# First graph layer: four fewer row blocks held on chip, eight gathers a block instead of seven, twelve row buffers

## The chip, the cores and the metric

The program runs on one core of a Trainium2 chip. The core has five engines that run side by side and meet through semaphores: TensorE (PE; its weight loads are listed as PEld), VectorE (DVE), ScalarE (ACT), GpSimd (POOL) and SyncE (SP). In this kernel SP issues the plain DMA transfers, and POOL issues the indirect ones, in which 128 row numbers choose 128 rows of a table. The metric is the time of one execution on the device in microseconds (us), the median of several executions. Lower is better.

## The reference, cut to what matters

The program is a stack of four graph layers over 6250 nodes of 256 values and 100000 edges. Only the first layer is touched:

```python
h = jnp.einsum('nd,od->no', x, W) + b          # one row of 256 values for each node
row, col = (edge_index[0], edge_index[1])      # src, dst
msgs = h[col]                                  # the row of each edge's dst ...
out = jax.ops.segment_sum(msgs, row, num_segments=h.shape[0])   # ... summed at its src
x = _layernorm(x + out, axis=-1)
```

The edges come sorted by `dst`, and `dst` is drawn as 6250 times the square of a uniform number, so that low node numbers have many more edges than high ones. `src` is uniform.

## The kernel before, in words

Nodes are cut into 49 blocks of 128. A first phase (`prepare`, up to about 900 us) computes `h`, splits each row into two halves of 32-bit values whose sum is the row (512 values, 2 KB), writes the table `rows0` to HBM, and keeps the rows of the first 20 node blocks on chip in the tile `first_rows` (`FIRST = 20`). It also sorts the edges by the block of their source. Each source block gets 17 tiles of 128 edge places (`S_TILES`), in the order of `dst`. As `dst` is sorted, tile t of a block can only hold targets from a known range of node blocks, its window (`WINDOWS`), worked out beforehand.

The first layer is `direct_l0` (L1173), which calls `by_source` (L1077). For each source block the 17 tiles fall into two kinds.

- Near tiles are the leading ones whose window ends at or below block `h` (`near_tiles`). Their target rows are on chip, so no row is fetched. PE builds, for each target block, a 128x128 matrix of how many edges lead from each source to each target: one bf16 product of two one-hot matrices for each pair of a tile and a target block (L1134). Four such matrices fill one PSUM tile `ps_q`, a quad, which ACT copies to SBUF as `a_hi` (L1137). Then each matrix is multiplied with the 128 kept rows, once for each half (L989 and L990 in `sum_halves`), into the sum `ps_g`.
- Far tiles are the rest. For each, POOL gathers the 128 rows of its edges from `rows0` into a buffer `g` by an indirect DMA (L983, called at L1157), and PE multiplies them with the one-hot matrix of the edges' sources, `cs`, again once for each half.

The one-hot matrices of block b+1 are made by DVE in `open_block` while block b is under way, in this order: `od` (one for each near tile, L1096), `os` and `cs` (one instruction each, L978). All three have two buffers, so that those of block b+1 have to wait until PE has used up those of block b-1. After them in DVE's order stand the layer's ends: the sum with `x` (L1186), the layer norm (L962 to L972) and the split into halves (L945).

The order is written out by hand (`manual_schedule`). The unit of work is one quad. PE builds the quad two units ahead of the one whose products it runs (`stages(len(units), 2, build, use)`). In each unit the far tiles due come first (`range(q * m // n_q, (q + 1) * m // n_q)` of m far tiles over n_q quads), then the products with kept rows. POOL's gathers are issued in the order in which PE uses them. A gather waits until its buffer is free, that is until PE has used the gather that had the buffer before, and until the gather eight before it has landed, for there are eight completion semaphores for POOL's transfers.

With `H0 = 24` as the bound for near tiles, the rows of blocks 20 to 23 are read back from `rows0` into a tile `more_rows` by one transfer of 1 MB at the start of the layer (L1176, L1177). By the windows, a source block then has 10 near and 7 far tiles, 59 pairs of tile and target block, 24 target blocks and 6 quads (the last block of 106 nodes: 8 near, 9 far, 52 pairs, 23 target blocks, 6 quads).

When the layer ends, the last rows it made are read back into `first_rows` for the second layer (L1776), and the second layer, `direct_l1`, begins. It, the third (`direct_l2`, which uses `by_source` with `exact` set and 16 buffers for gathered rows) and the fourth (`direct_l3`) gather rows at the same line L983.

Of the kernel before, what the change touches and what calls it, by code (L numbers as in the profile page):

```python
# [7 lines left out]
FT = mybir.dt.float32  # L8
# [8 lines left out]
P = 128  # L17
# [33 lines left out]
S_TILES = sum(n for _, _, _, n in STRETCHES)  # L51
TS = NB * S_TILES
S_ROWS = -(-(S_TILES * P * NB + E) // P)
H0, H1, H2, H3 = 24, 16, 9, 3
SURE = 3.5


# [31 lines left out]
FIRST = 20  # L89
# [6 lines left out]
W0 = 2 * D  # L96
# [555 lines left out]
class Slots:  # L652
# [40 lines left out]
    def hot(self, dst, b, lo, hi):  # L693
        self.k.nc.vector.tensor_scalar(dst, self.sb[:, lo:hi], float(b), None, op0=OP.is_equal)
# [54 lines left out]
class Scores:  # L749
# [46 lines left out]
    def load(self, c):  # L796
        if c % self.STEP and c != EC or c > EC or c in self.at:
            return
        at = self.at[c] = self.pool.tile([P, self.STEP, DE], FT, name="at", bufs=2)
        if c < EC:  # L800
            n = min(self.STEP, EC - c)
            self.k.nc.sync.dma_start(at[:, :n, :],
                                     self.attr[c * P:(c + n) * P, :].rearrange("(c p) d -> p c d", p=P))
        else:
            self.k.nc.sync.dma_start(at[:ET, 0, :], self.attr[P * EC:E, :])
# [142 lines left out]
def load_block(k, pool, table, b, name="xb", bufs=3):  # L948

    t = pool.tile([P, D], FT, name=name, bufs=bufs)  # L950
    n = rows_of(b)
    if n < P:
        k.nc.vector.memset(t, 0.0)
    k.nc.sync.dma_start(t[:n, :], table[b * P:b * P + n, :])
    return t
# [14 lines left out]
def normalized(k, dst, x, mv, rs):  # L970
    k.nc.vector.reciprocal(rs, rs)
    k.nc.vector.tensor_scalar(dst, x, mv[:, 0:1], rs, op0=OP.subtract, op1=OP.mult)  # L972


def one_hots(k, dst, loc, op=OP.is_equal):

    n = loc.shape[-1]
    k.nc.vector.tensor_tensor(dst, k.iota_row.unsqueeze(1).to_broadcast([P, n, P]),  # L978
                              loc.unsqueeze(2).to_broadcast([P, n, P]), op=op)


def gather(k, dst, table, idx):
    k.nc.gpsimd.indirect_dma_start(out=dst, out_offset=None, in_=table,  # L983
                                   in_offset=bass.IndirectOffsetOnAxis(ap=idx, axis=0))


def sum_halves(k, out, lhs, row, start, stop):

    k.nc.tensor.matmul(out, lhs, row[:, :D].bitcast(F32R), start=start, stop=False)  # L989
    k.nc.tensor.matmul(out, lhs, row[:, D:2 * D].bitcast(F32R), start=False, stop=stop)  # L990
# [16 lines left out]
class Pairs:  # L1007
# [30 lines left out]
    def by_source(self, t):  # L1038
        return self.s[:, t - self.t0, :]


def stages(n, lag, make, use):

    made = {}
    for i in range(n + lag):
        if i < n:
            made[i] = make(i)
        if i >= lag:
            use(i - lag, made.pop(i - lag))
# [27 lines left out]
def by_source(k, pool, psum, hot, h, table, width, idx, loc, rel, load, finish, scale=None):  # L1077

    nc = k.nc
    near = [Near(b, h) for b in range(NB)]
    units = [(b, q) for b in range(NB) for q in range(len(near[b].quads))]
    nn, nf = max(v.n for v in near), S_TILES - min(v.n for v in near)
    pairs = max(v.pairs for v in near)
    exact = scale is not None
    sides, far, sums, later = {}, {}, {}, []

    def open_block(b):
        v, s = near[b], b * S_TILES
        od = pool.tile([P, pairs * P], BF16, name="od", bufs=2)
        for t, (lo, hi) in enumerate(v.spans):
            o = (v.at[t] + lo) * P
            nc.vector.tensor_scalar(od[:, o:o + (hi - lo) * P], k.iota16[:, :(hi - lo) * P], rel[:, s + t:s + t + 1],  # L1096
                                    None, op0=OP.is_equal)
        os = pool.tile([P, nn, P], BF16, name="os", bufs=2)
        one_hots(k, os[:, :v.n, :], loc[:, s:s + v.n])
        by_s = [os]  # L1100
        if exact:
            by_s = []
            for i, w in enumerate(scale[1]):
                by_s.append(pool.tile([P, nn, P], BF16, name=f"osw{i}", bufs=2))
                ws = w[:, s:s + v.n].unsqueeze(2).to_broadcast([P, v.n, P])
                nc.vector.tensor_tensor(by_s[i][:, :v.n, :], os[:, :v.n, :], ws, op=OP.mult)
        sides[b] = od, by_s
        m = S_TILES - v.n
        if exact:
            far[b] = []  # L1110
            for t in range(v.n, S_TILES):
                far[b].append(pool.tile([P, P], FT, name="cs", bufs=2 * nf))
                nc.vector.tensor_scalar(far[b][-1], k.iota_row, loc[:, s + t:s + t + 1], scale[0][:, s + t:s + t + 1],
                                        op0=OP.is_equal, op1=OP.mult)
        else:
            cs = pool.tile([P, nf, P], F32R, name="cs", bufs=2)
            one_hots(k, cs[:, :m, :], loc[:, s + v.n:s + S_TILES])
            far[b] = [cs[:, j, :] for j in range(m)]

    def build(i):  # L1120
        b, q = units[i]
        v = near[b]
        if q == 0:
            load(b)
            if b + 1 < NB:
                open_block(b + 1)
        od, by_s = sides[b]
        pa = psum.tile([P, 4 * P], FT, name="ps_q", bufs=2 if exact else 5)
        n = len(v.quads[q])
        for j, d in enumerate(v.quads[q]):  # L1130
            steps = [(t, x) for t in v.of(d) for x in by_s]
            for m, (t, x) in enumerate(steps):
                o = (v.at[t] + d) * P
                nc.tensor.matmul(pa[:, j * P:(j + 1) * P], od[:, o:o + P], x[:, t, :], start=(m == 0),  # L1134
                                 stop=(m == len(steps) - 1))
        a = pool.tile([P, 4, P], FT if exact else F32R, name="a_hi", bufs=4)
        nc.scalar.copy(a[:, :n, :].rearrange("p j s -> p (j s)"), pa[:, :n * P])  # L1137
        return a

    def product(ps, a, row, start, stop):  # L1140
        if exact:
            nc.tensor.matmul(ps, a, row, start=start, stop=stop)  # L1142
        else:
            sum_halves(k, ps, a, row, start, stop)

    def use(i, a):
        b, q = units[i]
        v = near[b]
        if q == 0:
            sums[b] = psum.tile([P, D], FT, name="ps_g", bufs=2)  # L1150
        ps, m, n_q = sums[b], S_TILES - v.n, len(v.quads)
        if later:
            later.pop(0)()
        for j in range(q * m // n_q, (q + 1) * m // n_q):
            g = pool.tile([P, width], FT, name="g", bufs=16 if exact else 8)
            col = b * S_TILES + v.n + j
            gather(k, g, table, idx[:, col:col + 1])  # L1157
            product(ps, far[b][j], g, j == 0, False)
        ds = v.quads[q]
        for j, d in enumerate(ds):  # L1160
            product(ps, a[:, j, :], hot(d), False, q == n_q - 1 and j == len(ds) - 1)
        if q == n_q - 1:
            later.extend(finish(b, ps))
            del sides[b], far[b], sums[b]

    with k.tc.manual_schedule():
        open_block(0)
        stages(len(units), 2, build, use)
        for f in later:
            f()  # L1170


def direct_l0(k, pool, psum, a, hot, table, idx, loc, rel, keep, out_rows, out_x):  # L1173
    nc = k.nc
    made = {}
    more = pool.tile([P, H0 - FIRST, W0], FT, name="more_rows")  # L1176
    nc.sync.dma_start(more, table[FIRST * P:H0 * P, :].rearrange("(b p) d -> p b d", p=P))  # L1177

    def load(b):
        made[b, "x"] = load_block(k, pool, a["x"], b)  # L1180

    def finish(b, ps):
        y = made[b, "y"] = pool.tile([P, D], FT, name="y0", bufs=3)

        def add():
            nc.vector.tensor_add(y, made.pop((b, "x")), ps)  # L1186
            made[b, "ln"] = spread(k, pool, y)

        def norm():
            normalized(k, y, y, *made.pop((b, "ln")))  # L1190
            t = keep[:, b, :] if b < NA else pool.tile([P, W0], FT, name="hl", bufs=2)
            halves(k, t[:, :D], t[:, D:], y)
            store_block(k, out_rows, b, t, W0)
            store_block(k, out_x, b, y)

        return [add, norm]

    by_source(k, pool, psum, lambda d: hot[:, d, :] if d < FIRST else more[:, d - FIRST, :], H0, table, W0, idx, loc, rel, load, finish)


def direct_l1(k, pool, psum, a, rows_at, table, idx_d, loc_d, loc, rel, x_in, out_x):
# [942 lines left out]
```

## Time and profile before

| what | value |
|---|---|
| median of 3 executions | 4190.38 us (4179.15 to 4190.85) |
| the profiled execution: its time, its span | 4190.65 us, 4188.9 us |
| busy over the span: PE, DVE, POOL, ACT | 83%, 70%, 65%, 35% |
| first layer, first to last product | 929.9 to 1476.7 us |
| gathers at L983 with tables `rows` and list `idx_s` (first and fourth layer) | 1032, mean 1118 ns |
| HBM read, written | 486.32 MB, 62.09 MB |

Times in the profile count from the start of the span. PE's matmuls are pipelined: the recorded length of one overlaps the next, so the pace of PE is read from start to start. A gather at L983 in the rows of POOL is the time in which POOL makes the transfer's list of packets; the rows land later. "Idle before, releaser" says how long an engine stood still and what ended that. The view of the chain that ended last shows only shares of 0% for this program, so the stages are read one by one instead.

### The profile page before, as it was taken

The numbers are of one execution on the slowest core, as the hardware profiler recorded it, in microseconds if no ns is written. First come the engines' busy times: TensorE is split into PE (matmuls) and PEld (weight loads), VectorE is DVE, ScalarE is ACT, GpSimd is POOL, SyncE is SP. The second block draws the span as 40 slices with busy tenths as digits, with TensorE's granted clock in tenths as the row PEclk, the third lists the DMA queues.
The fourth block names the chain that finished last, engine by engine and source line by source line (L and its number), as shares of the span: only waits on it lengthen the run. The fifth ranks groups of instructions, "written<-read, shape, count | busy, mean of one in ns | idle before, by whom it ended". The sixth has DMA issues, their size and how long they took to land. (4 is left out here: it accounts for less than half of the span.)

```text
span 4188.9 us, 70909 instructions
## 1 busy us (share of the span) xinstructions
PE 3495.8 (83%) x23978; PEld 2791.3 (67%) x23988; DVE 2940.0 (70%) x9234; ACT 1474.3 (35%) x3780; POOL 2743.2 (65%) x2685
## 2 busy tenths in 40 slices
PE   7999999919999979888887999999754677777776
PEld 4666777619999967766665777777433565556565
DVE  8998776527776668887877555665396777777775
ACT  1444444403333312222221111111442555555554
POOL 2776666767767756566655777777104777777774
PEclk9999999959999989899998999999897888888888
DMA  4234333336767765466552333333254444444443
GB/s 83 70 104 104 104 96 98 83 67 209 215 215 213 216 205 149 142 179 184 157 172 83 109 108 109 108 109 108 50 124 120 132 138 132 143 136 134 142 136 90
DMA packets 373433, 552.45 MB, mean 132 GB/s; under 512 B 88710, under 2 KB 265064, under 8 KB 372774
## 3 DMA queue, kind: packets, MB, share of 16 engines
q0 software_dynamic: 136064, 353.87, 30.5%
q1 hardware_dynamic: 236998, 193.96, 15.7%
q8 instruction: 193, 3.16, 0.3%
q14 instruction: 178, 1.46, 0.1%
HBM read 486.32 MB, written 62.09 MB: 131 GB/s over the span
## 5 line engine op out<-in xcount | busy, mean ns | idle before, releaser
L983 POOL DMA_INDIRECT g<-rows,idx_s x1032 | 1154.1, 1118 | 390.6 <-issue 239.0
L933 POOL DMA_INDIRECT rec<-r_s,addr x590 | 588.9, 998 | 238.0 <-ACT r_s L833 112.4
L983 POOL DMA_INDIRECT g<-x,idx_s x541 | 556.9, 1029 | 221.1 <-issue 73.4
L983 POOL DMA_INDIRECT g<-rows,idx_d x383 | 430.3, 1124 | 275.4 <-PE ps_g L990 162.8
L828 PE MATMUL ps_b<-ew_w,a_t 128*128 128x257 f32 x1564 | 454.6, 407 | 0.0
L831 DVE SCALAR_TENSOR_TENSOR scr<-ps_b,a 128x256 bf16<-128x256 f32 x782 | 322.8, 423 | 167.1 <-PE ps_b L828 147.2
L1634 PE MATMUL ps_g<-g,s 128*128 128x257 f32 x1374 | 403.0, 463 | 0.0
L1134 PEld LDWEIGHTS <-od 128*128 128x128 bf16 x5947 | 348.7, 98 | 52.9 <-issue 19.8
L1634 PEld LDWEIGHTS ps_g<-g,s 128*128 128x128 f32 x1374 | 322.0, 238 | 62.4
L828 PEld LDWEIGHTS ps_b<-ew_w,a_t 128*128 128x128 f32 x1564 | 261.6, 190 | 106.0 <-issue 85.9
L1142 PE MATMUL ps_g<-g,cs 128*128 128x256 f32 x1082 | 289.9, 395 | 42.7 <-DMA g<-x,idx_s 41.6
L978 DVE TENSOR_TENSOR os<-iota_row,loc_s 128x768 bf16<-128x768 f32 (+3 forms) x294 | 271.9, 925 | 72.2 <-PE ps_q L1288 61.7
L1096 DVE TENSOR_SCALAR od<-iota,rel 128x128 bf16<-128x128 f16 (+9 forms) x780 | 247.9, 398 | 102.7 <-PE ps_q L1134 98.5
L833 ACT ACTIVATE r_s<-ps_b,half 128x1 f32<-128x1 f32 x782 | 204.5, 263 | 292.3 <-DVE scr L831 279.7
L1137 ACT CAST a_hi<-ps_q 128x512 fp32r<-128x512 f32 x294 | 172.4, 586 | 329.3 <-PE ps_q L1134 322.5
L1554 PE MATMUL ps_a<-ident,ep 128*128 128x128 f32 x833 | 155.3, 315 | 149.9 <-DVE ep L1543 99.6
L1137 ACT COPY a_hi<-ps_q 128x512 f32<-128x512 f32 x146 | 69.9, 479 | 590.7 <-PE ps_q L1134 571.4
L989 PE MATMUL ps_g<-g,cs 128*128 128x256 f32 x728 | 232.7, 336 | 48.1 <-DMA g<-rows,idx_d 46.2
L1142 PEld LDWEIGHTS ps_g<-g,cs 128*128 128x128 f32 x1082 | 186.3, 190 | 104.8 <-DMA g<-x,idx_s 84.0
L1291 ACT CAST a_hi<-ps_q 128x512 fp32r<-128x512 f32 x196 | 114.8, 586 | 383.1 <-PE ps_q L1288 382.9
L989 PE MATMUL ps_g<-first_rows,a_hi 128*128 128x256 f32 x980 | 245.6, 283 | 0.0
L990 PE MATMUL ps_g<-first_rows,a_hi 128*128 128x256 f32 x980 | 244.4, 282 | 0.0
(294 smaller groups left out, 8096.4 us busy)
## 6 DMA issues: line engine op xcount, KB each, us to landing
at<-in_edge_attr SPq DMA_DIRECT2D x65, 768.0 KB
edge_row<-node_row SPq DMA_DIRECT2D x49, 544.0 KB
xb<-x SPq DMA_DIRECT2D x144, 128.0 KB
g<-rows,idx_s POOLq DMA_INDIRECT x1032
xb<-in_x SPq DMA_DIRECT2D x96, 128.0 KB
x<-x SPq DMA_DIRECT2D x96, 128.0 KB
rows<-hl SPq DMA_DIRECT2D x47, 256.0 KB
rec<-r_s,addr POOLq DMA_INDIRECT x590
```

Of the source, the lines that this page charges most:

```text
L828: nc.tensor.matmul(z[:n_e, :], a_t[:, j * P:j * P + n_e], self.w, start=False, stop=True)
L831: nc.vector.scalar_tensor_tensor(scr[:n_e, :], z[:n_e, :D], 0.0, self.a[:n_e, :], op0=OP.max, op1=OP.mult, accum_out=s[:n_e, j:j + 1])
L933: s = nc.gpsimd.indirect_dma_start(out=self.table, out_offset=bass.IndirectOffsetOnAxis(ap=self.addr[:n, c:c + 1], axis=0), in_=self.rec[: ...
L978: k.nc.vector.tensor_tensor(dst, k.iota_row.unsqueeze(1).to_broadcast([P, n, P]), loc.unsqueeze(2).to_broadcast([P, n, P]), op=op)
L983: k.nc.gpsimd.indirect_dma_start(out=dst, out_offset=None, in_=table, in_offset=bass.IndirectOffsetOnAxis(ap=idx, axis=0))
L989: k.nc.tensor.matmul(out, lhs, row[:, :D].bitcast(F32R), start=start, stop=False)
L990: k.nc.tensor.matmul(out, lhs, row[:, D:2 * D].bitcast(F32R), start=False, stop=stop)
L1096: nc.vector.tensor_scalar(od[:, o:o + (hi - lo) * P], k.iota16[:, :(hi - lo) * P], rel[:, s + t:s + t + 1], None, op0=OP.is_equal)
L1134: nc.tensor.matmul(pa[:, j * P:(j + 1) * P], od[:, o:o + P], x[:, t, :], start=(m == 0), stop=(m == len(steps) - 1))
L1137: nc.scalar.copy(a[:, :n, :].rearrange("p j s -> p (j s)"), pa[:, :n * P])
L1142: nc.tensor.matmul(ps, a, row, start=start, stop=stop)
L1634: nc.tensor.matmul(ps, s[:, j, :], g[:, j, :D + 1], start=(j == 0), stop=False)
```

## The change

The tile `more_rows`, its transfer and the constant `H0` go. The bound for near tiles is `FIRST`, 20. The gathered rows of the first layer get 12 buffers instead of 8; four buffers of 2 KB for each partition are what `more_rows` took.

```diff
-H0, H1, H2, H3 = 24, 16, 9, 3
+H1, H2, H3 = 16, 9, 3
...
-            g = pool.tile([P, width], FT, name="g", bufs=16 if exact else 8)
+            g = pool.tile([P, width], FT, name="g", bufs=16 if exact else 12)
...
 def direct_l0(k, pool, psum, a, hot, table, idx, loc, rel, keep, out_rows, out_x):
     nc = k.nc
     made = {}
-    more = pool.tile([P, H0 - FIRST, W0], FT, name="more_rows")
-    nc.sync.dma_start(more, table[FIRST * P:H0 * P, :].rearrange("(b p) d -> p b d", p=P))
...
-    by_source(k, pool, psum, lambda d: hot[:, d, :] if d < FIRST else more[:, d - FIRST, :], H0, table, W0, idx, loc, rel, load, finish)
+    by_source(k, pool, psum, lambda d: hot[:, d, :], FIRST, table, W0, idx, loc, rel, load, finish)
```

By the windows, a source block now has 9 near and 8 far tiles, 47 pairs, 19 target blocks and 5 quads (the last block: 7 near, 10 far, 39 pairs, 18 target blocks, 5 quads). Over the layer the pairs go from 2884 to 2295, the matrices of kept rows from 1175 to 930, the quads from 294 to 245, and the gathers from 345 to 394.

## The prediction

> **What bounds the kernel now.** The change touches one stage, so I read the busy time by stretch first. The first layer runs from 929.9 to 1476.5 us; the third, from 2240 us, uses the same helper. Columns: length, busy time of PE, PEld, DVE, ACT, POOL (instructions), granted clock, DMA share, GB/s.
>
> ```profile
> 929.90:1476.50 546.60, 545.78 (x5924) 533.04 (x5923) 375.47 (x851) 202.31 (x391) 383.29 (x337) 1.00 0.69 212
> ...
> 2240.00:2935.00 695.00, 656.74 (x5096) 540.83 (x5094) 419.54 (x1072) 96.83 (x213) 536.43 (x521) 1.00 0.38 108
> ```
>
> PE has no gap in the first layer. Second, the costliest groups there (busy us, mean ns, then idle before and its releasers), and third who waited for whom in it:
>
> ```profile
> L983 POOL DMA_INDIRECT g<-rows,idx_s x337 | 383.3, 1137 | 161.2 <-PE ps_g L990 102.0 <-issue 48.9 <-PE ps_q L1134 10.3
> L978 DVE TENSOR_TENSOR os<-iota_row,loc_s 128x1280 bf16<-128x1280 f32 (+1 forms) x47 | 69.3, 1475 | 0.0
> L978 DVE TENSOR_TENSOR cs<-iota_row,loc_s 128x896 fp32r<-128x896 f32 (+1 forms) x47 | 51.0, 1085 | 0.4 <-PE ps_g L990 0.4
> ```
> ```profile
> POOL g L983 <- PE ps_g L990: 102.0, 150, 9.9
> ...
> PE ps_q L1134 <- ACT node_row L1475: 1.3, 1, 1.3
> ```
>
> POOL waits for PE to free row buffers; PE waits once, 1.3 us at the start, and (last fence) 0.81 us at the end. So PE bounds this stage. Fourth, the order of time on PE (start, length, instruction), which gives its pace:
>
> ```profile
> 1001.16 0.84 PE L1134 MATMUL ps_q<-os,od 128*128 128x128 bf16 x12
> 1001.82 0.36 PE L989 MATMUL ps_g<-g,cs 128*128 128x256 f32 x1
> 1002.02 0.28 PE L990 MATMUL ps_g<-g,cs 128*128 128x256 f32 x1
> 1002.13 0.28 PE L989 MATMUL ps_g<-first_rows,a_hi 128*128 128x256 f32 x1
> ```
>
> Twelve pair products take 0.66 us (0.055 each), a row product 0.12, the first row product after pair products 0.20. Fifth, POOL:
>
> ```profile
> 923.08 0.94 POOL L983 DMA_INDIRECT g<-rows,idx_s  x1 [0.30 <-issue]
> 933.96 0.95 POOL L983 DMA_INDIRECT g<-rows,idx_s  x1 [9.94 <-PE ps_g L990]
> ...
> 1052.10 1.25 POOL L983 DMA_INDIRECT g<-rows,idx_s  x1 [0.67 <-PE ps_g L990]
> 1054.03 2.25 POOL L983 DMA_INDIRECT g<-rows,idx_s  x1 [0.68 <-PE ps_g L990]
> 1056.58 0.95 POOL L983 DMA_INDIRECT g<-rows,idx_s  x1 [0.30 <-issue]
> ```
>
> An undisturbed gather takes 0.95 us and 0.30 us pass before the next: a step of 1.25 us. The long ones recur once a block (2.28 us at 1042.92, 2.25 at 1054.03: the block's period is 11.11 us). DVE in those moments:
>
> ```profile
> 1049.64 3.42 DVE L1096 TENSOR_SCALAR od<-iota,rel 128x128 bf16<-128x128 f16 x10 [1.74 <-PE ps_q L1134]
> 1052.98 1.48 DVE L978 TENSOR_TENSOR os<-iota_row,loc_s 128x1280 bf16<-128x1280 f32 x1
> 1054.38 1.08 DVE L978 TENSOR_TENSOR cs<-iota_row,loc_s 128x896 fp32r<-128x896 f32 x1
> ```
>
> The gather begun at 1054.03, inside `os`, ends at 1056.28, 0.82 us after `cs` ends: it stood still while DVE ran instructions with two inputs from SBUF. I call this lost time of POOL S, us a block.
>
> **The change, part by part.** PE a block: pairs 59 to 47, row products 62 to 54 (24+7 to 19+8, two each), switches from pair to row products 6 to 5 at 0.08. Before: 59×0.055 + 62×0.12 + 6×0.08 = 11.17 us (the period measured is 11.11). After: 2.59 + 6.48 + 0.40 = 9.47. PE's bound falls by about 49×1.65 = 81 us. But POOL then has 8 gathers a block: 8×1.25 + S = 10.0 + S. Even with S = 0 that is above 9.47, so **POOL becomes the bound** and the PE saving is worth only what POOL allows.
>
> The POOL chain: the eighth gather starts at 923.08, and with 12 buffers the next four need no PE, so the idle 9.94 us goes: the ninth starts at 924.33. The 394th starts 385 steps later, 481.3 us, at 1405.6, plus 47 S (blocks 0 and 1 were opened before). From the last gather's start to PE's last product took 1476.68 − 1467.60 = 9.1 us before, including a landing slowed by the second layer's loads; I keep it. Stage end: 1414.7 + 47 S, against 1476.7.
>
> S before: (1137 − 947)×337 = 64.0 us over 48 blocks, 1.33 a block (947 ns is the median gather), while the two-input instructions of DVE (`os` 69.3, `cs` 51.0, the splits at L945 12.3 and 8.1 us) took 140.7 us: 0.455 us lost for each us of them. Afterwards `os` has 9 tiles, 1.475×0.9 = 1.33 us, `cs` 8, 1.085×8/7 = 1.24, the split 0.43: 3.0 a block as before, so by this row S = 1.36. In the third layer, where POOL already runs gathers end to end, the loss is smaller; in the fourth, with one 2.4 us instruction of this kind a block (L1522, 113.7 us in all; L1650 20.9 and L1651 20.8), it is larger:
>
> ```profile
> L983 POOL DMA_INDIRECT g<-x,idx_s x521 | 536.4, 1030 | 158.7 <-issue 68.2 <-PE ps_g L1142 64.0 <-DMA g<-x,idx_s 13.1
> ```
> ```profile
> L983 POOL DMA_INDIRECT g<-rows,idx_s x647 | 710.8, 1099 | 197.1 <-issue 176.1 <-PE ps_g L1634 4.9 <-PE ps_a L1554 4.0
> ```
>
> Third: (1030−947)×521 = 43.2 us over 173.8 us of `osw` and `os`, 0.25, S = 0.74. Fourth: 98.3 over 155.4, 0.63, S = 1.89. I take S = 1.2: near the same stage's row, a little lower, because `cs` of block b+1 must wait for the last far product of block b−1, which in a gather-bound stage comes late; that pulls `os` and `cs` apart, and the third layer's shorter holds cost less. Stage end: 1414.7 + 56.4 = 1471.1, **−5.6 us**.
>
> The tail: the second layer begins after 20 loads on SP's queue. Before, 7 came after the last store; the last DVE wait on them ended at 1489.46. In the new instruction order 9 come after it:
>
> ```profile
> 1480.46 6.78 SPq L1776 DMA_DIRECT2D first_rows<-rows  x7
> ```
> ```profile
> 1475.46 0.39 PE L989 MATMUL ps_g<-g,cs 128*128 128x256 f32 x1 [0.81 <-DMA g<-rows,idx_s]
> ```
>
> At 6.78/7 = 0.97 us each, two more add **+1.9 us** (bounds 0, if landings cover it, and 1.9).
>
> At nothing: 49 fewer ACT copies (0.587 us each) and one `od` fewer a block, both on engines that had gaps (202 and 375 of 547 us busy); the 1 MB transfer of `more_rows`, for PE's start hung on `node_row`; 49 more gathers of 256 KB, 12.8 MB, which lift 212 GB/s by about 11% and the DMA share from 0.69 to 0.77. The bound of eight gathers in flight needs a landing slower than 8 steps, 10 us; the last gather, ended at 1468.55, was used at 1475.46, so landing took at most 6.9 us there. The other layers keep their instructions; their cost change lies between 0 and what a shifted start could do, taken as 0.
>
> Sum: −5.6 + 1.9 = −3.7 us on the profiled 4190.65: **4187 us** (the median is 0.3 us lower, no matter). With S = 0.74: −27.2 + 1.9, 4165. With S = 1.89: +26.8 + 1.9, 4219.
>
> **The rivals.** *Gathers run as in the third layer* (S at or below 1.01): faster, 4165 to 4178. For it: there POOL was saturated too. Against: its holds are 0.95 us, shorter than a gather's step; `os` and `cs` here are 1.33 and 1.24, so each nearly always catches one.
>
> *DVE and POOL lock into a bad phase* (S of 1.55 or more): slower. When `os` starts hangs on PE, PE hangs on a landed gather, so the same place in the gather sequence can be hit in each block. Caught at the start of `os`, a gather loses most of 1.33 us, the next caught by `cs` most of 1.24; at S = 1.89 4219. For it: before, 2.2 us gathers recur block after block. Against: landings vary, which moves the phase. It decides from S = 1.28 on (no gain), and by 0.3% from 1.55.
>
> *PE stays the bound and all 81 us come* (4110): needs gathers under 9.47/8 = 1.18 us a step; no row shows one under 1.25. Dropped to 1 in 100.
>
> *`od` blocks gathers too*: then S gains up to nine instructions, about 2.8 us, a block, +132 us, 4319. Against: the gathers at 1049.24 and 1050.48 kept 0.94 us under `od`; only one of the three beside it stretched, to 1.25. The Trainium skill (SBUF — State Buffer, the box on the "DVE blocks DMA" trap and "Who interferes with whom") states this rule: while DVE runs a one-input instruction in a mode that uses both its port pairs, GpSimd cannot write the descriptors of its transfers. By the two short gathers it does not hold as stated; 2 in 100.
>
> *The half clock*: PE would idle about 15%; in the second layer, busy 599 of 690 us, the clock was 0.92. Then 9.47/0.92 = 10.3, still under POOL's 11.2: no price.
>
> **How the numbers follow.** 0.3% of 4190 is 12.6 us, about what can be told from no change. With the tail, faster by more needs S below 1.01: 0.28 (the 0.01 of full gain in it). Slower by more needs S above 1.55: 0.28 (0.02 of `od` in it). Between, the likeliest: 0.44, with its own range 4178 to 4203. The range reaches to a tenth on each side, 4166 to 4215, near both S bounds.
>
> **What would show it.** Right: PE gets waits for `g` landings, some 1.5 us a block; POOL's idle before L983 falls to 0.30 us a gather; the period is near 11.2 us; gathers 9 to 12 start by 930 us. The mean gather tells S: 947 ns + S/8. Wrong: POOL still waiting for `ps_g`, `od` stretching gathers, or a period off 10.7 to 11.9 us.

## The result, and the profile after

| | before | after |
|---|---|---|
| median of 11 executions each, taken in turn on one chip | 4188.41 us (4179.15 to 4192.15) | 4174.92 us (4166.73 to 4180.86) |
| the profiled execution | 4190.65 us | 4166.73 us |
| first layer, end of PE's last product | 1476.7 us | 1459.4 us |
| second layer, first instruction of DVE | 1489.46 us | 1471.62 us |

The ratio of after to before is 0.9972, with a 95% interval of 0.9962 to 0.9982: by it the change wins 0.28%, 11.7 us; the medians lie 13.5 us apart. The profiled pair differs by 24 us. Of these, 17.3 are there when the first layer ends, 1.0 of them already when it begins (PE's first product starts at 928.9 us, before at 929.9), and 0.6 lie between the layers. The other 6 lie behind, where no instruction was changed; the executions of either kernel spread over 13 to 14 us, and the pair takes one near the top of before and the lowest of after. So I read causes from the first layer alone and sizes from the medians. That the other executions lost as much in their gathers as the profiled one is not shown.

The busy time of the first layer after the change (columns: stretch, length, busy time and instructions of PE, PEld, DVE, ACT, POOL, granted clock, DMA share, GB/s):

```profile
927.00:1460.00 533.00, 483.29 (x4943) 465.30 (x4942) 359.82 (x806) 167.99 (x343) 402.64 (x383) 0.97 0.78 241
```

PE, which had no gap before, now stands still for 49.7 us of this stretch; 2.5 of them lie ahead of its first product and behind its last, which leaves 1.0 us a block. The groups of the same stretch (busy us, mean ns of one, idle before with its releasers):

```profile
L983 POOL DMA_INDIRECT g<-rows,idx_s x383 | 403.1, 1053 | 122.4 <-PE ps_g L990 42.6 <-issue 34.7 <-DMA g<-rows,idx_s 22.8
...
L978 DVE TENSOR_TENSOR os<-iota_row,loc_s 128x1152 bf16<-128x1152 f32 (+1 forms) x47 | 63.0, 1340 | 0.0
L978 DVE TENSOR_TENSOR cs<-iota_row,loc_s 128x1024 fp32r<-128x1024 f32 (+1 forms) x47 | 57.9, 1232 | 65.3 <-PE ps_g L990 65.2
```

POOL's idle time is 122.4/383 = 0.32 us a gather, hardly more than the bare step between two of them. But for one wait at the start, POOL runs from the first gather to the last without a break that it could lose. The loss over an undisturbed gather is (1053 − 947)×383/47 = 0.86 us a block; that is S, which the prediction took as 1.2. And who waited for whom:

```profile
DVE cs L978 <- PE ps_g L990: 65.2, 46, 4.0
PEld ps_g L989 <- DMA g<-rows,idx_s: 52.8, 31, 3.0
PE ps_g L989 <- DMA g<-rows,idx_s: 46.4, 29, 2.8
POOL g L983 <- PE ps_g L990: 42.6, 121, 5.6
```

PE waits for gathered rows, which it never did before but for the last. `cs` waits for PE 46 times, 1.4 us each: before, it followed `os` at once. POOL's 42.6 us on `ps_g` are 120 short ones of some 0.3 us, which is the step itself, and one of 5.6 us at the start:

```profile
926.53 0.95 POOL L983 DMA_INDIRECT g<-rows,idx_s  x1 [0.31 <-issue]
933.09 0.94 POOL L983 DMA_INDIRECT g<-rows,idx_s  x1 [5.61 <-PE ps_g L990]
```

Here twelve gathers are out by 927.5 us, and the thirteenth has to wait until PE, which begins at 928.9, has used up the first.

How a gather loses its time is seen in the order of time on POOL and DVE, some blocks later:

```profile
1113.59 0.95 POOL L983 DMA_INDIRECT g<-rows,idx_s  x1 [0.30 <-issue]
1114.84 1.26 POOL L983 DMA_INDIRECT g<-rows,idx_s  x1 [0.30 <-PE ps_g L990]
1116.41 0.96 POOL L983 DMA_INDIRECT g<-rows,idx_s  x1 [0.31 <-PE ps_q L1134]
1117.67 1.27 POOL L983 DMA_INDIRECT g<-rows,idx_s  x1 [0.30 <-PE ps_g L990]
```
```profile
1112.27 3.01 DVE L1096 TENSOR_SCALAR od<-iota,rel 128x128 bf16<-128x128 f16 x9 [0.26 <-PE ps_q L1134]
1115.21 1.34 DVE L978 TENSOR_TENSOR os<-iota_row,loc_s 128x1152 bf16<-128x1152 f32 x1
1116.90 1.22 DVE L978 TENSOR_TENSOR cs<-iota_row,loc_s 128x1024 fp32r<-128x1024 f32 x1 [0.35 <-PE ps_g L990]
```

`cs` ends at 1118.13 and the gather begun under it at 1118.95, 0.82 us later. `os` ends at 1116.55, and the gather begun at 1116.41 ends at 1117.37, again 0.82 later. The gather begun at 1114.84 shows the same thing without a two-input instruction: it began under the last `od`, which ends at 1115.28, and it ends at 1116.10, 0.82 us behind that `od` and 0.45 us before `os` is through. The gather begun at 1113.59, among the shorter `od` before it, kept 0.95 us.

Going through the stretch from 940 to 1450 us in this way, a gather ends 0.80 to 0.83 us behind 46 of 46 `os` and 46 of 47 `cs`. Of these 92, 33 began when at most 0.15 us of the instruction was left, and lost next to nothing (they are 0.94 to 0.97 us long). Of the 60 that began under an `os` or a `cs` with more than that to go, 59 end so behind it: the instruction sets when such a gather ends. Of the 85 gathers that were already under way when one of them started, none ends so behind it. And 43 gathers end as far behind an `od`, 42 of them behind one of the two longest of a block (0.51 and 0.54 us). Sorted by the instruction behind which they end, the gathers lose 0.36 us a block to `cs`, 0.18 to `os` and 0.26 to `od`. What one gather loses depends on how much of the instruction is left when it begins; by these rows the worst case under `os` would be 1.34 + 0.82 = 2.16 us in all. Where the gathers begin against DVE's instructions is what I mean by phase from here on.

The seam to the second layer, on SP's queue and on DVE:

```profile
1463.17 9.21 SPq L1774 DMA_DIRECT2D first_rows<-rows  x9
```
```profile
1471.62 0.96 DVE L978 TENSOR_TENSOR os<-iota_row,loc_s 128x768 bf16<-128x768 f32 x1 [9.22 <-DMA first_rows<-rows]
```

The nine loads take 9.21 us on SP against 6.78 for seven, and yet the second layer begins 12.2 us after PE's last product, against 12.8 before; its first instruction starts before the nine are through.

### The profile page after: what moved, and what is told of

Read it like the earlier page. It is cut to its first block, busy times and chain, and to the rows that moved or that the text cites. A ratio compares the mean times of both kernels' runs of the same rounds, so it can differ in the third digit from the quotient of the medians.

```text
span 4164.9 us, 68897 instructions
## 1 busy us (share of the span) xinstructions
PE 3430.7 (82%) x23007; PEld 2718.9 (65%) x23007; DVE 2923.5 (70%) x9185; ACT 1440.9 (35%) x3731; POOL 2768.2 (66%) x2734
## 5 line engine op out<-in xcount | busy, mean ns | idle before, releaser
L983 POOL DMA_INDIRECT g<-rows,idx_s x1081 | 1173.3, 1085 | 352.9 <-issue 226.1
L1134 PEld LDWEIGHTS <-od 128*128 128x128 bf16 x5358 | 319.9, 99 | 53.1 <-issue 21.8
L1142 PE MATMUL ps_g<-g,cs 128*128 128x256 f32 x1082 | 290.9, 396 | 45.3 <-DMA g<-x,idx_s 44.3
L989 PE MATMUL ps_g<-g,cs 128*128 128x256 f32 x777 | 243.4, 333 | 93.6 <-DMA g<-rows,idx_s 46.4
L1137 ACT CAST a_hi<-ps_q 128x512 fp32r<-128x512 f32 (+2 forms) x245 | 138.4, 565 | 345.8 <-PE ps_q L1134 341.1
L1096 DVE TENSOR_SCALAR od<-iota,rel 128x768 bf16<-128x768 f16 (+3 forms) x731 | 225.4, 383 | 35.3 <-PE ps_q L1134 31.0
L1289 ACT CAST a_hi<-ps_q 128x512 fp32r<-128x512 f32 x196 | 114.9, 586 | 376.5 <-PE ps_q L1286 376.2
L1286 PE MATMUL ps_q<-od,os 128*128 128x128 bf16 (+3 forms) x1222 | 213.8, 291 | 29.8 <-DVE od L1026 15.6
L1026 DVE TENSOR_SCALAR od<-iota,rel 128x512 bf16<-128x512 f16 (+2 forms) x929 | 238.2, 307 | 0.0
```

Source lines behind the costliest of these rows:

```text
L1026: k.nc.vector.tensor_scalar(self.d[:, o * P:(o + hi - lo) * P], k.iota16[:, (lo - w) * P:(hi - w) * P], rel[:, s + t:s + t + 1], None, op0 ...
L1286: nc.tensor.matmul(pa[:, (d - d0) * P:(e - d0) * P], p.by_source(t), p.by_target(t, d, e - d), start=(m == 0), stop=(m == len(p.tiles) - 1 ...
```

## The experiments

My theory after the result: the gathers on POOL are the bound, and S, the time that they lose, is the only large number left; I put it down to the two-input instructions. The rivals were that PE, the landings or DVE as a whole set the pace. Each kernel was timed beside executions of the kernel before (their medians lay at 4193.02, 4186.48 or 4185.5 us), so kernels are best compared through their ratios to it.

### The twelve buffers

```diff
-            g = pool.tile([P, width], FT, name="g", bufs=16 if exact else 12)
+            g = pool.tile([P, width], FT, name="g", bufs=16 if exact else 8)
```

> The changed kernel with 8 row buffers instead of 12. Theory: the first layer runs at the pace of POOL's gathers, 1.25 us each plus the time they stand still for DVE's two-input instructions, so buffers matter only at the start, where 12 let four more gathers run before PE begins. Without them the stage ends 4 x 1.25 = 5 us later: about 4180 us, 8 us below the kernel before. Rival: the buffers carry the gain (POOL waits for PE in every block, as before): back at 4188 us or above, and POOL's idle time before its gathers for ps_g near 100 us again.

Measured: 4177.1 us, ratio to before 0.9966 (0.9952 to 0.9979), against 0.9972 (0.9962 to 0.9982) with twelve. The four extra buffers bring nothing that can be told, and the rival, that they carry the gain, is out: POOL's idle time for `ps_g` is 55.5 us, not 100. They do change the start: with eight, POOL waits for PE after the eighth gather, and the ninth comes when the thirteenth came with twelve.

```profile
933.24 0.94 POOL L983 DMA_INDIRECT g<-rows,idx_s  x1 [15.35 <-PE ps_g L990]
```

That is four steps behind, 4×1.25 = 5 us once in the layer; the medians show 2 us, inside their uncertainty. In the profiled execution, which took 6 us more than the median of its kernel, the first layer ended 11.7 us later than with twelve: 5.8 us at the thirteenth gather and the rest later, where the gathers lost 0.95 us a block. So a gain of the buffers of some 5 us is neither shown nor excluded. Later on both kernels are gather-bound, and no run shows that buffers make gathers shorter.

### One gather a block less

The last far tile of a block is multiplied with the rows of the gather before it, so the sum is not the layer's; PE's work is that of the changed kernel, POOL's is seven gathers.

```diff
-            g = pool.tile([P, width], FT, name="g", bufs=16 if exact else 12)
-            col = b * S_TILES + v.n + j
-            gather(k, g, table, idx[:, col:col + 1])
+            if exact or j < m - 1:
+                g = pool.tile([P, width], FT, name="g", bufs=16 if exact else 12)
+                col = b * S_TILES + v.n + j
+                gather(k, g, table, idx[:, col:col + 1])
+                last[0] = g
+            g = last[0]
```

> The changed kernel with seven gathers a block instead of eight; the last far tile of a block is multiplied with the rows of the gather before it, so that part of the sums is left wrong and PE's work stays the same. Theory: with 7 x 1.25 + 0.8 = 9.6 us for POOL and 9.5 us for PE a block the period falls from 11.1 to about 9.7 us: 65 us below the changed kernel, about 4110 us. Rival (something else, such as landings or DVE, sets the pace): less than 20 us.

Measured: 4111.7 us, ratio 0.98 (0.9784 to 0.9817), 81 us under before, and 63 under after by the medians, 72 by the ratios. PE is busy again nearly throughout:

```profile
1130.00:1230.00 100.00, 100.00 (x1078) 97.72 (x1076) 80.99 (x179) 36.64 (x75) 77.49 (x74) 1.00 0.81 250
```

So the 81 us of saved PE work, which the prediction counted, are real, and the eighth gather takes most of them back.

### An eighth gather for the kernel before, twice

First with a buffer from the common ring:

```diff
             product(ps, far[b][j], g, j == 0, False)
+            if not exact and j == 3:
+                g = pool.tile([P, width], FT, name="g", bufs=8)
+                gather(k, g, table, idx[:, col:col + 1])
```

> The kernel before with one more gather in each block, whose rows nobody uses; PE's work is unchanged. Theory: POOL's 8 x 1.25 us plus 0.9 to 1.3 us lost to DVE make 10.9 to 11.3 us against PE's 11.1 us a block, so the added gather costs between 0 and 12 us in all: 4188 to 4200 us. Rival (a gather costs its full step on the path already): 48 x 1.25 = 60 us, 4248 us.

Measured: 4283.0 us, ratio 1.0209 (1.0192 to 1.0226), +90 us, outside of what either theory expected. The experiment was badly built: nothing reads that buffer, so its next user waits not for PE but for the unread rows to land.

```profile
POOL g L983 <- DMA g<-rows,idx_s: 75.0, 45, 3.2
```

A landing stood in POOL's chain once a block. It says nothing on the theory. The second try gives the extra gather a tile of its own, so that it waits only for its own landing of a block earlier, and seven buffers to the others:

```diff
-            g = pool.tile([P, width], FT, name="g", bufs=16 if exact else 8)
+            g = pool.tile([P, width], FT, name="g", bufs=16 if exact else 7)
...
+            if not exact and j == 3:
+                g2 = pool.tile([P, width], FT, name="g2", bufs=1)
+                gather(k, g2, table, idx[:, col:col + 1])
```

> The kernel before with an eighth gather a block into a tile of its own that nothing reads (seven row buffers and this one, so that it waits only for its own landing of a block earlier, which is long done). It leaves TensorE's work as it was. Theory (the changed kernel's time is that of eight gathers a block, 8 x 1.05 + 8 x 0.30 = 10.8 to 11.2 us a block, and TensorE's work of before is 11.1): the same as before or a little over, 4188 to 4205 us. Rival (an eighth gather lengthens every block by its own 1.25 us whatever TensorE does): 47 x 1.25 = 59 us more, 4247 us.

Measured: 4207.9 us, ratio 1.0055 (1.0039 to 1.0072), +21 us. The 59 us of the rival did not come; the theory's upper end was missed by 3 us. The groups show why:

```profile
L983 POOL DMA_INDIRECT g<-rows,idx_s x384 | 428.5, 1116 | 127.7 <-issue 78.3 <-PE ps_g L990 33.0 <-PE ps_q L1134 14.9
```

The mean gather is 1116 ns here, S = 8×0.169 = 1.35 us, so eight gathers take 8×(0.947 + 0.305) + 1.35 = 11.37 us a block, above PE's 11.11. POOL is the bound even here, by a little: (11.37 − 11.11)×48 = 12 us, and in the profiled execution, the shortest of four, the stage ended 15 us later than before. The expectation had put the mean at 1053 ns, the changed kernel's. S is not carried from one kernel to the next.

### Less work for PE

The products of the second halves of the kept rows are left out in the first layer (19 products of 0.12 us a block, 2.3 us), so the sums miss the low halves of the kept rows.

```diff
-                product(ps, a[:, j, :], hot(d), False, q == n_q - 1 and j == len(ds) - 1)
+            if exact:
+                product(ps, a[:, j, :], hot(d), False, q == n_q - 1 and j == len(ds) - 1)
+            else:
+                nc.tensor.matmul(ps, a[:, j, :], hot(d)[:, :D].bitcast(F32R), start=False,
+                                 stop=q == n_q - 1 and j == len(ds) - 1)
```

> The changed kernel without the second product (the low half) of each kept row block in the first layer, so its sums lack those low halves; 19 products of 0.12 us a block go. Theory (POOL sets the pace): PE idles more and the time stays within 5 us of the changed kernel, about 4175 us. Rival (PE still sets the pace of a good part of the blocks): up to 48 x 2.3 = 110 us less, 4065 us.

Measured: 4201.71 us, ratio 1.0015 (1.0004 to 1.0026): 2.3 us of PE work less a block, and yet 18 us more than the changed kernel by the ratios, 27 by the medians. The cause stands in the gathers:

```profile
L983 POOL DMA_INDIRECT g<-rows,idx_s x382 | 427.5, 1119 | 124.9 <-issue 50.0 <-DMA g<-rows,idx_s 31.4 <-PE ps_g L990 23.4
```

S is (1119 − 947)×8 = 1.38 us, 0.52 more than in the changed kernel, and 47×0.52 = 24 us. No instruction of DVE or POOL was touched. What PE's work does touch is the moments at which it frees `os` and `cs`, and with them the phase: a block now loses 0.53 us behind `os` where it lost 0.18, 0.57 behind `cs` instead of 0.36, and 0.09 behind `od` instead of 0.26. This is the mechanism of the prediction's rival of a bad phase. PE's granted clock also fell in this stretch, from 0.97 to 0.92; PE stands still for a quarter of it, so its pace does not bound, but no run separates the two.

### The two-input instructions themselves

This measures the disputed cost directly: `os` and `cs` of the first layer are built tile by tile by a one-input instruction from the fp16 counter row, as `od` is. It gives DVE 2.7 us a block more to do.

```diff
-        one_hots(k, os[:, :v.n, :], loc[:, s:s + v.n])
+        if exact:
+            one_hots(k, os[:, :v.n, :], loc[:, s:s + v.n])
+        else:
+            for t in range(v.n):
+                nc.vector.tensor_scalar(os[:, t, :], k.iota16[:, :P], loc[:, s + t:s + t + 1], None, op0=OP.is_equal)
...
-            one_hots(k, cs[:, :m, :], loc[:, s + v.n:s + S_TILES])
+            for j in range(m):
+                nc.vector.tensor_scalar(cs[:, j, :], k.iota16[:, :P], loc[:, s + v.n + j:s + v.n + j + 1], None,
+                                        op0=OP.is_equal)
```

> The changed kernel, with the first layer's one-hot tiles (os and cs) built tile by tile by a tensor_scalar from the fp16 iota instead of by one tensor_tensor with two inputs in SBUF each. Theory (the gathers are the chain, and what they lose over 947 ns each is mostly lost to the two two-input instructions of a block): the mean gather falls from 1053 ns towards 975 ns, so 47 blocks x 8 x 0.078 = 29 us less, about 4146 us; VectorE has 9 x 0.29 + 8 x 0.33 instead of 2.57 us a block to do, 7.5 + 2.7 = 10.2 us a block, close to the gathers' 8 x (0.975 + 0.30) = 10.2, so a part of the gain can be lost to waits for VectorE: 4146 to 4165 us. Rival (the gathers lose their time to whatever VectorE does, by its busy time): the mean gather goes up, VectorE being busy for 2.7 us a block more: above 4180 us. Rival (what is lost comes from the rows' landings and not from VectorE): no change of the mean gather, 4175 us within 5.

Measured: 4146.39 us, ratio 0.9908 (0.9892 to 0.9925), against 4146 expected. This version beats both kernels: 0.9% under before, and by the two ratios 0.64% under after.

```profile
L983 POOL DMA_INDIRECT g<-rows,idx_s x382 | 377.1, 987 | 127.7 <-issue 43.9 <-PE ps_g L990 39.6 <-DMA g<-rows,idx_s 27.5
```
```profile
L1122 DVE TENSOR_SCALAR cs<-iota,loc_s 128x128 fp32r<-128x128 f16 x378 | 80.7, 304 | 35.0 <-PE ps_g L990 34.2
L1103 DVE TENSOR_SCALAR os<-iota,loc_s 128x128 bf16<-128x128 f16 x421 | 76.1, 297 | 0.0
```

The mean gather falls from 1053 to 987 ns, S from 0.86 to 0.32, although DVE is busier (78.2 of 100 us from 1130 us on, against 68.8). DVE's busy time as such does not hold gathers, and the landings do not either. Of the 54 gathers that began under a one-input `os` with more than 0.15 us to go, none was held; 25 end behind a one-input `cs`, which costs 0.04 us a block, and 28 behind an `od`, 0.13. The Trainium skill (SBUF — State Buffer, "Who interferes with whom") states that a VectorE instruction with two inputs in SBUF contends with a GpSimd instruction that reads SBUF; the drop of S by 0.54 us agrees. The same section says that one-input instructions in a two-port mode shut GpSimd out for their whole length; as far as `od` is in such a mode, the 43 gathers that end behind one in the changed kernel agree. With 17 more one-input instructions a block in place of two long ones the loss fell all the same, so short ones cost little here.

Only `cs` in this form, `os` left as it is:

> As the one before, but only cs is built tile by tile (VectorE 7.5 + 8 x 0.33 - 1.23 = 8.9 us a block, clear of the gathers' 10.2). Theory: cs held the gathers for about 0.36 of the 0.86 us a block, so 47 x 0.36 = 17 us less than the changed kernel, about 4158 us, and a mean gather of 1008 ns. Rival (by VectorE's busy time): 4180 us or more. Rival (the landings): 4175 us within 5.

Measured: 4172.28 us, ratio 0.9966 (0.9954 to 0.9977), no gain that can be told over after, where 17 us were expected. The time alone would fit the rival of the landings, but the gathers did change:

```profile
L983 POOL DMA_INDIRECT g<-rows,idx_s x382 | 408.6, 1070 | 124.1 <-issue 41.4 <-PE ps_g L990 35.5 <-DMA g<-rows,idx_s 35.3
```

The mean rose from 1053 to 1070 ns with one two-input instruction a block instead of two. Sorting each gather longer than 0.965 us by the instruction behind which it ends: in the changed kernel `cs` costs 0.36 us a block and `os` 0.18, in this one `os` costs 0.70. A gather ends 0.8 us behind each of 46 `os`, and the mean length of these is 1651 ns against 1140. With `cs` gone, `os` came to stand at a worse place. My expectation had taken the shares as fixed to the instructions, and they are not.

Only `os` in this form, `cs` left as it is:

> The counterpart of the run with only cs built tile by tile: here only os is, and cs stays one two-input instruction of 1.23 us a block. In the changed kernel, gathers that end 0.82 us behind the end of cs lost 0.49 us a block and those behind os 0.35; with cs gone, os came to stand worse against the gathers and lost 0.90, so the sum of both did not fall. Theory (one two-input instruction a block is enough to hold a gather, and how much it holds is a matter of where it falls against the gathers: between 0.1 and 1.2 us for cs in the runs so far): the mean gather between 960 and 1100 ns, the time between 4140 and 4195 us, and almost all that is lost stands in gathers that end 0.82 us behind a cs. Rival (each of the two costs a fixed share, os 0.35): 47 x 0.35 = 16 us less than the changed kernel, 4158 us.

Measured: 4161.7 us, ratio 0.9944 (0.9923 to 0.9964), mean gather 1037 ns; `cs` costs 0.45 us a block, `od` 0.25, as in the changed kernel. The expectation's 0.49, 0.35 and 0.90 give to `cs` and `os` every long gather that overlaps them, also those that end behind an `od`; by the ends they are 0.36, 0.18 and 0.70. Within a few us the time fits both expectations, so this run does not tell them apart; the one with `cs` did.

The same edit in the kernel before:

> The kernel before with the same edit of os and cs. Theory: TensorE is the bound there (no idle time between its instructions), so faster gathers buy nothing: 4188 us within 6, unless VectorE's 10 us a block come to be late for TensorE's 11.1. Rival (the gathers were late there as well, and the change's gain came from something else than the order of bounds): as many us less as in the changed kernel, 4160 to 4170 us.

Measured: 4181.47 us, 0.5 us below the expected band, ratio 0.9989 (0.998 to 0.9999). There the gathers got shorter too, from 1137 to 1009 ns, more than in the changed kernel, and it bought 5 us (0.4 to 8 by the interval):

```profile
L983 POOL DMA_INDIRECT g<-rows,idx_s x337 | 339.9, 1009 | 208.3 <-PE ps_g L990 186.1 <-issue 19.2 <-PE ps_q L1140 3.1
```
```profile
1130.00:1230.00 100.00, 100.00 (x1093) 97.69 (x1091) 76.98 (x298) 37.73 (x72) 63.20 (x64) 1.00 0.71 214
```

PE is busy for all of the 100 us, and POOL's time saved turns up as waiting for PE: 186.1 us against 102.0. The order of bounds in the two kernels is what the prediction had read from the profile.

Last, the edit of `os` and `cs` in the first layer, and of `os` in the third layer as well:

> First layer as in the run with os and cs both tile by tile (4146 us), and in the third layer os as well (its two weighted copies osw stay two-input instructions, 0.95 us each). Theory: TensorE waits for gathers' landings for 37 us in the third layer's 600 us, and two of the three two-input instructions of a block stay, so at most a third of the gathers' loss of 0.74 us a block goes, 47 x 0.25 = 12 us: 4135 to 4150 us. Rival (VectorE, with 6 x 0.29 in the place of 0.95 us a block, comes late for TensorE there): 4150 to 4180 us.

Measured: 4139.54 us, ratio 0.9894 (0.9875 to 0.9913), the lowest of the versions that compute the layer in full; its interval overlaps that of the first layer's edit alone, so a gain from the third layer is not shown. The mean gather in the third layer is 1032 ns against 1037, and PE's waits for landings there 43.9 us against 37.1.

### What the runs say together

The step from a mean gather to the stage's end is 47×8 = 376 gathers. Against the changed kernel (1053 ns; its last product with kept rows starts at 1459.1 us):

| first layer of | mean gather, ns | 0.376 × difference, us | last product with kept rows, us | difference, us |
|---|---|---|---|---|
| both one-input | 987 | −24.8 | 1433.3 | −25.8 |
| `os` one-input | 1037 | −6.0 | 1452.3 | −6.8 |
| `cs` one-input | 1070 | +6.4 | 1464.7 | +5.6 |
| fewer products on PE | 1119 | +24.8 | 1485.8 | +26.7 |

Four changes of DVE's and PE's work, and in each the stage moves by what its gathers gained or lost, within 2 us. The column of starts is from the rows of the product's line, for the changed kernel and for the one with both edits:

```profile
L990 PE MATMUL ps_g<-first_rows,a_hi x930: 274/283/415, 932.8 to 1459.1; 128*128 128x256 f32 x186
```
```profile
L990 PE MATMUL ps_g<-first_rows,a_hi x930: 277/283/415, 932.2 to 1433.3; 128*128 128x256 f32 x186
```

## Why the prediction was right or wrong

The predicted 4187 us lies 12 us above the 4174.92 measured, with the range holding it. By the ratio, −0.28%, the change falls just inside the likeliest case, "within 0.3%"; by its time it lies 3 us below that case's 4178 to 4203, where the prediction gave 0.28. That it came out on the border of two cases is the work of S, which was taken too large.

- **PE bounds before, POOL after: right.** PE has gaps now, POOL has none after the start. The block's period came to 10.9 us (381 gathers in 517.7 us), where 11.2 was forecast. The 81 us of PE's work are there when the eighth gather goes (4111.7 us), and shorter gathers are worth 5 us before and 28 us after.
- **The POOL chain's start: wrong by about 4 us.** The step "with 12 buffers the next four need no PE, so the idle 9.94 us goes" moved the wait instead of removing it. POOL fills twelve buffers by 927.5 us, before PE has begun, and then waits 5.61 us for the first to come free, 0.30 of which are the step. The eighth gather had also come 1.5 us earlier, so 5.6 − 0.3 − 1.5 = 3.8 us are to be added.
- **S: the term that was mis-sized.** It was taken as 1.2 us a block and is 0.86. 47×0.34 = 16 us, the largest part of the miss. The prediction charged all of S before to the two-input instructions, at 0.455 us for each us of them; sorted by their ends, the gathers before lost 0.96 us a block to `cs`, 0.11 to `os` and 0.26 to `od`. The reason given for going below the same stage's row was right: `cs` now waits 1.4 us for the last far product and no longer follows `os` at once, and the gathers of 2.2 us, which before came behind both in one, became two of 1.14 and 1.32 us in the mean. Its effect was taken too small: `cs` fell from 0.96 to 0.36, `os` rose to 0.18, and `od` stayed at 0.26. By the numbers, the rival "gathers run as in the third layer" (S at or below 1.01, 4165 to 4178 us) described the case better than the forecast did.
- **The sum.** The step from gather to gather, S left out, was 1.253 us where 1.25 was taken, +1.0 us over 381 steps, and the last gather's start to PE's end, kept at 9.1 us, was 8.6. −5.6 + 3.8 − 16.0 + 1.0 − 0.5 = −17.3 us for the stage, as measured.
- **The tail, +1.9 us: did not come.** It hung on the last loads being the last wait. The two more loads did take 2.4 us more on SP, but the second layer started before they were all through: the lower bound, 0, was the value.
- **A bad phase: the mechanism is there.** The prediction put it at 0.28 and priced it by the fourth layer's row. It did not fall to the changed kernel, but an experiment with fewer products on PE came near its bound of 1.55 (S 1.38), and a one-input `cs`, which was to lower S, raised it to 0.98. S came out between 0.72 and 1.38 in kernels that kept one or both two-input instructions, so a forecast to better than some tenths of a us was hardly to be had from the trace of before. The range held the time because it was built on the bounds of S, the term that did vary; where in it the kernel would come to lie, the trace of before did not tell.
- **`od` blocks gathers: true in kind, a tenth of its price.** Gathers that end 0.82 us behind an `od` lose 0.26 us a block before the change and 0.26 after; the rival had put it at 2.8. Of the two gathers of 0.94 us on which the prediction dropped it, the first was under way before the first `od` began, and the second began 0.1 us before the end of a short one; the third, of 1.25 us, begun at 1052.10, ended 0.82 us behind the second longest `od` of its block.

What sets the phase in a given kernel is open. It follows from when PE frees the buffers of `os` and `cs`, which follows from when gathers land; no run here fixed it from outside. Also open is the 6 us that the profiled pair differs by after the first layer, and whether the `os` of the third layer is worth its edit. And since no run has a one-input instruction as long as `os` or `cs`, these runs do not tell whether it is their second input or their length that makes them cost the most.

## What to carry to other kernels

When a change takes work off the bound, work out the next bound's pace before counting the gain: here 81 us were freed, and one more transfer a block took back all but 13. A stall that comes from two engines meeting is not a price for each instruction: measure it in the kernel at hand, and rather take away the form of instruction that causes it than shift it, for a shift (less work on PE, one of the two instructions gone) can make it worse. And extra buffers move a start-up wait to a later transfer; whether they shorten it depends on when the first one comes free.

## What was not expected of the hardware

- A gather that begins under `os` or `cs` with more than 0.15 us of it to go ends 0.81 to 0.83 us after that instruction does, in 59 of 60 cases in the changed kernel, however early in it the gather began. One that is already under way is not held. A gather without such a neighbour takes 0.947 us in all.
- Not only two inputs hold a gather, and not every instruction does. Counting gathers begun under an instruction with more than 0.15 us to go, from 940 to 1450 us, in all runs but the one with the unread buffer: 359 of 362 end 0.80 to 0.83 us behind a one-input `od` of about 0.5 us, but none of 72 behind the layer norm's statistics (L962, 0.43 us), none of 76 behind the sum with one operand in PSUM (`y<-xb,ps_g`, 0.41 us) and none of 153 behind a one-input `os` (0.30 us).
- Building eight one-hot tiles by eight instructions of 0.304 us instead of one of 1.23 us doubles VectorE's time for them (2.4 us) and makes the layer faster, when the tiles of `os` are built so too.
- Taking 2.3 us of work a block off PE made the program slower by 0.4% against the changed kernel, by the ratios 1.0015 and 0.9972.
